# Gated cross-attention and mixture of experts on one core: token normalisation on ScalarE, and another order for the sixth and seventh batch

## The chip, the core and the metric

The kernel runs on one core of a Trainium2 chip. The core has TensorE (PE, matrix products, with a weight load of its own, PEld), VectorE (DVE), ScalarE (ACT), GpSimd (POOL) and SyncE (SP), which issues most DMAs. Each engine takes its instructions in program order and waits on semaphores for the others. Matrix products land in PSUM. The metric is the device time in microseconds of one execution, as the median of several runs. The program is all in fp32.

## The reference

`x` and `ctx` hold 8 batches of 256 rows with 512 columns. The rows are the channels of the attention and the tokens of the experts.

```python
x = x + tanh(g_xattn) * attention(layernorm(x), ctx, ctx)   # 16 heads of 16 channels, 512 positions, rotary
x = x + tanh(g_ffn) * moe(layernorm(x))                     # 8 experts, top 2 per token, hidden size 1024
# moe, per token:
#   logits = x @ gate_w ; top-2 softmax gives two weights
#   out = sum over the two experts of weight * ((silu(x @ w0[e]) * (x @ w1[e])) @ wo[e])
```

`layernorm` has no learned scale: it subtracts the mean over the 512 columns and divides by the root of variance plus 1e-5.

## The kernel before

**Attention.** A batch has 16 heads, taken in 4 units of 4 heads, and each unit goes through 4 blocks of 128 positions: a batch is 16 *steps*, and the attention has 128 steps, 0 to 127, written out by hand. In a step PE makes two groups of scores (`scores`, L551: four matmuls in each), whose maxima DVE takes (L559), and, five steps later (`LAG`), the scores again, transposed and less the maximum (`exponentials`, L590), of which ACT takes the exponential (L597). Both kinds use three PSUM buffers `s` in turn. A third product (`attend`, L607) sums values by exponentials. A scheduler holds a table `beside` of all other work: `do(step, place, fn, ...)` puts a function into a step at place 0, 1 or 2. For every step the program emits place 0, one group of exponentials and one of scores, place 1, the second group of each, and place 2. After step 127 only exponentials and what is left over are emitted, up to step 133.

`run` emits the entries of one place: products first, each then followed by its evacuation from PSUM, and the other functions after that. All products of this kind share one PSUM bank, `m`, of which there is one buffer: the next place's product waits until the last one has been evacuated by ACT or DVE.

**A batch's other work.** Let `t` be the batch's first step. Before it come the loads of `x` and `ctx` (`loads`, on SP's queue; `x` has three buffers, so the load waits until the batch three before has been normalised for its tokens), the mean and variance of `x` on DVE (`query_stats`), the normalisation for the query (`query_norm`; POOL computes the factors `rstd` and `less` in `Norm.scales`, and applies them, but for the first batch DVE applies them), products for k and q (`turn`, evacuated by ACT as `straight`), a swap of neighbouring rows by DMA on SP's queue, and the rotation on POOL (`rotate`). With `s = t + 24`, after the batch's last unit, follow `merge` (the output product, in halves of 256 columns; ACT scales it, POOL adds it to `x`, SP stores it), `token_stats` at s+5 (DVE statistics, POOL's `scales`), `token_norm` at s+6 (L160 on DVE, one 128x512 tile in each of two places, into `pay`, which has one buffer), `token_turn` (transposes, evacuated by ACT as `hT`), `choose` (logits) and the router: ten pieces (`largest`, `first_of`, `compare`, `count`, `shares`, `weigh`, `send`), nearly all small DVE instructions, the last of which scatter token rows with POOL's indirect DMAs into `rows`, sorted by expert.

The lists of strings such as `"9.1 11.1 13.1 14.1 ..."` give step after `s` and place of the two token turns, the logits and the ten pieces of the router. Batches 0 to 4 have them spread over s+9 to s+19. Batch 5 (the sixth, the last that "early" rows need) has them between s+9 and s+14, steps 113 to 118; batch 6 (the seventh) between s+9 and s+13, steps 129 to 133.

**Early rows.** At step 119 `start_early` loads the first 432 rows of expert 0, which batches 0 to 5 have filled, and clears four tiles `y` on DVE. `turn_early` transposes them in four pieces. After the attention the last batch is finished and routed while a generator (`go`) fills PE with matmuls of expert 0 on these rows. A loop for overflowing rows follows (it runs for no rows or few, but all engines meet there), then the gathers of the sums so far into `y`, and the experts' products, which are the second half of the span.

Of the kernel before, what the change touches and what calls it, by code (L numbers as in the profile page):

```python
# [8 lines left out]
FP = mybir.dt.float32  # L9
AF = mybir.ActivationFunctionType  # L10
ALU = mybir.AluOpType
# [3 lines left out]
P = 128  # L15
B, C, N = 8, 256, 512
# [5 lines left out]
CC = C // P  # L22
NCH = N // P
UNITS = 2 * NG
E, M = 8, 1024
# [11 lines left out]
AHEAD, EARLY, LATE = 6, 432, 160  # L37
# [3 lines left out]
ROW = N + 1 + E  # L41
# [8 lines left out]
def gated_cross_attention_moe(  # L50
# [89 lines left out]
    class Norm:  # L140


        def __init__(self, pool, part, srcs):
            self.srcs = srcs
            self.mv = pool.tile([P, CC, 2], FP, tag="mv" + part, name="mv")
            self.st = [pool.tile([P, 6], FP, tag=f"st{part}{c}", name="st") for c in range(CC)]
            self.rstd = pool.tile([P, CC], FP, tag="rstd" + part, name="rstd")
            self.less = pool.tile([P, CC], FP, tag="less" + part, name="less")

        def stats(self, c):  # L150
            nc.vector.bn_stats(self.st[c], self.srcs[c])
# [2 lines left out]
        def scales(self):  # L154
            nc.gpsimd.tensor_scalar(self.rstd, self.mv[:, :, 1], EPS, None, ALU.add)
            nc.gpsimd.tensor_tensor(self.rstd, self.rstd, neg_half, ALU.pow)
            nc.gpsimd.tensor_scalar(self.less, self.mv[:, :, 0], -1.0, None, ALU.mult)

        def apply(self, eng, dst, c):
            eng.tensor_scalar(  # L160
                dst, self.srcs[c], self.less[:, c : c + 1], self.rstd[:, c : c + 1], ALU.add, ALU.mult
            )

    w_even = ctx.enter_context(tc.tile_pool(name="w_even", bufs=1))

# [161 lines left out]
    with ExitStack() as fill:  # L327
# [79 lines left out]
        def bank():  # L407


            if not banks:  # L410
                banks.append(ps_1.tile([P, N], FP, tag="m", name="m"))
            return banks[0]
# [13 lines left out]
        def full(fn, *args):  # L426

            run([(fn, (*args, h)) for h in range(2)])
# [33 lines left out]
        def query_norm(b):  # L462
            xns[b] = r1.tile([P, CC, N], FP, tag="xn", name=f"xn{b}")
            norms[b].scales()
            for c in range(CC):
                norms[b].apply(nc.gpsimd if b else nc.vector, xns[b][:, c, :], c)

        def loads(b):
            load_x(b)
# [93 lines left out]
        def turn_half(src, h, at=None):  # L563

            ps = bank()[:, halves[h if at is None else at]]
            for i in range(2):
                nc.tensor.transpose(ps[:, i * P : (i + 1) * P], src(2 * h + i), ident)
            return ps
# [72 lines left out]

            return later

        def turn_back(b, g, h):
            ps = turn_half(lambda i: outs[b, g][:, i].rearrange("p j q d -> p (j q d)"), h)

            def later():
                if h == 0:
                    ats[b, g] = p1.tile([P, N], FP, tag=f"at{g}", name="at")
                nc.scalar.copy(ats[b, g][:, halves[h]], ps)  # L650

            return later
# [35 lines left out]

        def token_norm(b, c):
            if c == 0:  # L690
                pays[b] = p1.tile([P, CC, ROW], FP, tag="pay", name="pay")
            norms[b].apply(nc.vector, pays[b][:, c, :N], c)

        hTs = {}

# [18 lines left out]
        routes = {}  # L714


        def choose(b, c):
            lg = bank()[:, halves[c]][:, :E]
            hT = hTs.pop(c)
            for d in range(DC):  # L720
                nc.tensor.matmul(
                    lg,
                    lhsT=hT[:, d, :],
                    rhs=gw[:, d, :],
                    start=(d == 0),
                    stop=(d == DC - 1),
                )

            def later():
                if c == 0:  # L730
                    routes[b] = {"vals": small("logits", [P, CC, E])}
                nc.vector.tensor_copy(routes[b]["vals"][:, c, :], lg)

            return later
# [121 lines left out]
        def do(step, place, fn, *args):  # L856
            beside.setdefault((step, place), []).append((fn, args))
# [4 lines left out]
        for b in range(B):  # L862
            t = b * per_batch


            if b:
                do(t - 19, 1, loads, b)
                for c in range(CC):
                    do(t - 17, 1 + c, query_stats, b, c)
                do(t - 17, 2, query_norm, b)  # L870
                first = (-12, -10, -3, -1) if b == 1 else (-14, -12, -3, -1)
                for i, name_g in zip(first, group_turns):
                    for h, cols in enumerate(halves):
                        do(t + i + h, 2, turn, b, *name_g, cols)
                for i, name_g in zip((-4, -3, 4, 5), group_turns):
                    do(t + i, 2, rotate, b, *name_g)
            at = (2, 2, 3, 4) if b == 0 else (-8, -7, -6, 1) if b == 1 else (-10, -9, -8, 1)
            for mc, i in enumerate(at):
                if b:
                    do(t + i, 2, values, b, mc, halves[0])  # L880
                else:
                    do(i, 1 if mc == 3 else 2, values, b, mc, halves[mc == 1])
            for w in range(UNITS):
                u = UNITS * b + w
                s = t + w * NCH
                for mc in range(NCH):
                    do(s + LAG + 1 + mc, 1, attend, u, mc)
                for h in range(2):
                    do(s + NCH - 1 + h, 2 - h, lower, u, h)
                    if u + 1 < UNITS * B:  # L890
                        do(s + LAG + 5, 1 + h, normalise, u, h)
                        if w % 2:
                            do(s + LAG + 6 + h, 1 + h, turn_back, b, w // 2, h)
            if b + 1 == B:
                break
            s = t + per_batch + LAG + 3
            for c in range(CC):
                for h, cols in enumerate(halves):
                    do(s + 1 + 2 * c + h, 2, merge, b, c, cols)
                do(s + 5, 1 + c, token_stats, b, c)  # L900
                do(s + 6, 1 + c, token_norm, b, c)
            if b + 2 == B:
                at = "9.1 9.2 11.1 11.2 12.1 12.1 12.2 12.2 13.1 13.2 13.2 13.2 13.2"
            elif b + 1 == AHEAD:
                at = "9.1 11.1 11.2 12.1 12.1 12.2 12.2 12.2 13.1 13.2 13.2 14.1 14.1"
            else:
                at = "9.1 11.1 13.1 14.1 14.2 15.1 15.2 16.2 17.1 17.2 18.1 18.2 19.1"
            at = [(s + int(i[:-2]), int(i[-1])) for i in at.split()]
            for i, piece in zip(at, ((token_turn, b, 0), (token_turn, b, 1), (choose, b))):
                if b + 1 < AHEAD:  # L910
                    later = 1 if piece[0] is token_turn and piece[2] else 0
                    for h in range(2):
                        do(i[0] + h * later, 1 + h, *piece, h)
                else:
                    do(*i, full, *piece)
            for i, (fn, *args) in zip(at[3:], router):
                do(*i, fn, b, *args)
        do(-5, 2, turn, 0, "k", 0, whole)
        for c in range(CC):
            do(-5, 2, query_stats, 0, c)  # L920
# [19 lines left out]
        def start_early():  # L940
            prep.close()
            pool = fill.enter_context(tc.tile_pool(name="early", bufs=1, side="right"))
            early["pool"] = pool
            early["sg"] = fill.enter_context(tc.tile_pool(name="early_sg", bufs=2, side="right"))
            nc.vector.tensor_scalar(taken[:, 0:1], taken[:, 0:1], float(EARLY), None, ALU.max)
            early["rows"] = Rows(pool, 0, EARLY)
            early["y"] = [
                pool.tile([P, N], FP, tag=f"y{j}", name="y") for j, _ in early["rows"].tiles
            ]
            for y in early["y"]:  # L950
                nc.vector.memset(y, 0.0)

        do(t - 1, 1, start_early)
        def turn_early():
            banks.clear()
            early["rows"].turn(bank, nc.scalar.copy)

        for at in ((t + 5, 1), (t + 5, 2), (t + 11, 2), (t + 12, 2)):
            do(*at, turn_early)

        held = []
# [26 lines left out]
        with tc.manual_schedule():  # L988
# [31 lines left out]
            go(1)  # L1020
            full(token_turn, b, 1)
            go(1)
            full(choose, b)
            for fn, *args in router:
                if fn is count:
                    go(4)
# [79 lines left out]
        late_p = ctx.enter_context(tc.tile_pool(name="late", bufs=1, reuse_waits="tile"))  # L1106
        fx = ctx.enter_context(tc.tile_pool(name="fx", bufs=2, reuse_waits="tile"))
        with tc.manual_schedule():
            early["rows"].residuals(early["y"])
            ws_next = matrices(1, w_odd)  # L1110
            late = Rows(late_p, EARLY, LATE)
            following = Rows(fx, ROWS, CAP)
            for _ in work:
                pass
            late.turn_all(get_x, nc.vector.tensor_copy)
# [107 lines left out]
```

## Time and profile before

| what | value |
|---|---|
| median of 3 runs | 1432.69 us (1431.8 to 1433.01) |
| profiled execution | 1431.27 us, span 1429.6 us |
| mean granted TensorE clock | 0.987 |
| PE busy | 1380.8 us, 97% of the span |
| DVE, ACT, POOL busy | 581.4, 412.1, 309.6 us |
| first scores (step 0) | 19.73 us after the start |
| last step with scores (127) starts | 640.15 us |
| first early matmul | 667.04 us |
| PE continues behind the overflow loop | 703.93 us |

A row of the timeline gives the start, the duration, engine, line, operation, the tiles written and read, their shape, how many like instructions were merged, and in brackets how long the engine stood idle before it and what released it. A row of the waits gives engine and line that waited, on what, the total, how many times, and the longest. A row of busy times of a stretch gives its bounds and length, then PE, PEld, DVE, ACT and POOL busy with the number of instructions, the granted clock, the share of DMA and GB/s.

### The profile page before, as it was taken

To read this page: it belongs to the slowest core of one execution; us is meant where nothing else is said; L and a number is where in the kernel's file an instruction comes from. 1 tells how busy PE (TensorE), PEld (TensorE's weight loads), DVE (VectorE), ACT (ScalarE), POOL (GpSimd) and SP (SyncE) were. 2 spreads that over 40 slices of the span, in tenths; PEclk is the share of its full clock that TensorE was granted. 3 is DMA by queue.
4 is the path that set the end of the run, shared out by engine and by line. 5 is a ranking of instruction groups with operands and counts; after the bars stand their busy time and mean duration, and the time that the engine had idled before them with its cause. 6 is when DMAs were issued, how large, how long until landed. Compare 5 with 4: busy or idle time off the path is not lost. (4 is left out here: it accounts for less than half of the span.)

```text
span 1429.6 us, 18158 instructions
## 1 busy us (share of the span) xinstructions
PE 1380.8 (97%) x7380; PEld 766.2 (54%) x7380; DVE 581.4 (41%) x1058; ACT 412.1 (29%) x617; POOL 309.6 (22%) x361
## 2 busy tenths in 40 slices
PE   5999999999999999998999999999999999999996
PEld 2333343434434343333447876858768577585772
DVE  5666767686767777672313111121211211112110
ACT  1556555555555555354100100101001010010000
POOL 6231515243341415211201102011020110100101
PEclk9999999999999999899999999999999999999998
DMA  6600512021111101010354234033340332310100
GB/s 216 216 19 23 175 69 88 16 65 40 46 52 46 52 16 61 25 47 38 145 180 150 80 125 141 1 141 128 118 133 17 140 128 103 121 47 16 43 1 28
DMA packets 49061, 117.76 MB, mean 82 GB/s; under 512 B 6122, under 2 KB 7146, under 8 KB 48976
## 3 DMA queue, kind: packets, MB, share of 16 engines
q1 hardware_dynamic: 40688, 91.26, 18.3%
q0 software_dynamic: 8288, 25.32, 4.9%
q8 instruction: 59, 0.97, 0.3%
q14 instruction: 26, 0.21, 0.0%
HBM read 78.51 MB, written 30.91 MB: 77 GB/s over the span
## 5 line engine op out<-in xcount | busy, mean ns | idle before, releaser
L559 DVE TENSOR_REDUCE nm<-s 128x2 f32<-128x1024 f32 x256 | 312.9, 1224 | 145.2 <-PE s L551 142.2
L597 ACT ACTIVATE e<-s 128x1024 f32<-128x1024 f32 x256 | 261.2, 1023 | 190.1 <-PE s L551 148.7
L551 PE MATMUL s<-k,q 32*128 32x512 f32 x1024 | 288.9, 651 | 6.9 <-POOL q L508 6.1
L590 PE MATMUL s<-qa,k 32*128 32x512 f32 x1024 | 287.1, 649 | 0.0
L257 PE MATMUL u<-hT,w 128*128 128x272 f32 (+1 forms) x960 | 233.4, 387 | 1.5 <-DVE act L271 1.5
L257 PE MATMUL g<-hT,w 128*128 128x272 f32 (+1 forms) x960 | 233.4, 387 | 0.0
L270 ACT ACTIVATE sg<-g 128x272 f32<-128x272 f32 (+1 forms) x120 | 46.8, 391 | 611.5 <-PE g L257 608.0
L287 PE MATMUL po<-wo,act 128*32 128x128 f32 (+1 forms) x976 | 221.0, 427 | 0.0
L271 DVE TENSOR_TENSOR act<-sg,u 128x272 f32<-128x272 f32 (+1 forms) x120 | 51.4, 429 | 368.4 <-PE u L257 368.4
L257 PEld LDWEIGHTS g<-hT,w 128*128 128x128 f32 x960 | 179.4, 190 | 37.2 <-issue 2.9
L257 PEld LDWEIGHTS u<-hT,w 128*128 128x128 f32 x960 | 179.4, 190 | 36.6 <-DVE act L271 1.7
L306 POOL DMA_INDIRECT out_x<-y,xt x41 | 39.6, 967 | 570.7 <-DVE y L298 532.8
L287 PEld LDWEIGHTS po<-wo,act 128*32 128x32 f32 (+1 forms) x976 | 99.3, 148 | 102.5 <-issue 102.3
L607 PE MATMUL av<-e,vones 128*32 128x512 f32 x1024 | 139.0, 615 | 0.0
L590 PEld LDWEIGHTS s<-qa,k 32*128 32x128 f32 x1024 | 76.8, 185 | 74.7 <-issue 64.1
L298 DVE SCALAR_TENSOR_TENSOR y<-po,xt,y 32x128 f32<-32x128 f32 (+1 forms) x61 | 32.8, 538 | 180.5 <-PE po L287 180.2
L551 PEld LDWEIGHTS s<-k,q 32*128 32x128 f32 x1024 | 76.9, 186 | 17.1 <-ACT e L597 7.4
L607 PEld LDWEIGHTS av<-e,vones 128*32 128x32 f32 x1024 | 20.3, 109 | 98.9 <-issue 98.9
L677 POOL TENSOR_TENSOR x<-x,mrg 128x512 f32<-128x512 f32 x14 | 17.9, 1276 | 200.0 <-ACT mrg L673 200.0
L238 POOL DMA_INDIRECT y<-out_x,xt x41 | 40.9, 997 | 68.4 <-issue 32.3
L257 PE MATMUL s<-hT,w 128*128 128x432 f32 x128 | 48.4, 529 | 2.4 <-DVEq L1051 2.4
L489 ACT ACTIVATE straight<-m,col 128x256 f32<-128x256 f32 (+1 forms) x60 | 29.3, 489 | 68.7 <-DVE o L635 24.3
(135 smaller groups left out, 995.8 us busy)
## 6 DMA issues: line engine op xcount, KB each, us to landing
w<-in_w SPq DMA_DIRECT2D x16, 2048.0 KB, 10.4
wo<-in_wo SPq DMA_DIRECT2D x8, 2048.0 KB, 9.4
rows<-nobody SPq DMA_DIRECT2D x8, 1042.0 KB, 7.3
xt<-rows SPq DMA_DIRECT2D x32, 260.5 KB, 4.7
swapped<-straight SPq DMA_DIRECT2D x64, 128.0 KB, 2.0
ctx<-in_kv SPq DMA_DIRECT2D x8, 512.0 KB, 4.3
x<-in_x SPq DMA_DIRECT2D x16, 256.0 KB, 2.8
out_x<-x SPq DMA_DIRECT2D x16, 256.0 KB, 2.0
```

The source lines that it names most:

```text
L238: gather = nc.gpsimd.indirect_dma_start(out=y[: at.shape[0], :], out_offset=None, in_=out_rows, in_offset=bass.IndirectOffsetOnAxis(ap=at, ...
L257: nc.tensor.matmul(ps[:, :step], lhsT=w[:, d, mc * P : (mc + 1) * P], rhs=self.hT[:, d, lo : lo + step], start=(d == 0), stop=(d == DC - 1),)
L270: nc.scalar.activation(sg, gu[0][:, :step], AF.Silu)
L271: nc.vector.tensor_tensor(self.act[:, mc, lo : lo + step], sg, gu[1][:, :step], ALU.mult)
L287: nc.tensor.matmul(po[i * space : i * space + n, :w], lhsT=self.act[:, mc, j * P : j * P + n], rhs=wout[:, mc, i * w : (i + 1) * w], start ...
L298: nc.vector.scalar_tensor_tensor(part, po[i * space : i * space + n, :w], wt[:n, j, :], part, ALU.mult, ALU.add,)
L306: scatter = nc.gpsimd.indirect_dma_start(out=out_rows, out_offset=bass.IndirectOffsetOnAxis(ap=self.ids[j], axis=0), in_=y[:n, :], in_offs ...
L551: nc.tensor.matmul(ps[:, j, :], lhsT=q[sl, i * P : (i + 1) * P], rhs=k[sl, :], start=True, stop=True,)
L559: nc.vector.tensor_reduce(nm[:, i, at : at + SLOT + 1 : SLOT], ps, AX.X, ALU.max, negate=True)
L590: nc.tensor.matmul(ps[:, j, :], lhsT=ks[u][sl, mc * P : (mc + 1) * P], rhs=qas[u][sl, :], start=True, stop=True,)
L597: nc.scalar.activation(es[u, mc][:, 2 * jp : 2 * jp + 2, :], ps, AF.Exp, scale=float(HD**-0.5))
L607: nc.tensor.matmul(avs_[u][slot(j), :], lhsT=vones[b % 2][:, mc, g * HG + 2 * j + par, :], rhs=e[:, j, :], start=(mc == 0), stop=(mc == NC ...
```

## The change

- `Norm` computes one factor more on POOL, `bias` = `less` x `rstd`, and `apply` on ACT is an Identity activation with that bias and `rstd` as scale.
- `token_norm` goes from DVE to ACT, and from s+6 to s+7. The first batch's `query_norm` goes from DVE to ACT as well; those of the other batches stay on POOL. `pay` gets two buffers.
- `loads`, `query_stats` and `query_norm` of batches 1 to 7 come two steps later (`t`-17 and `t`-15).
- Batch 5's token turns, logits and router get the steps that batches 0 to 4 have, with the two sends at s+19 and s+20 (steps 123, 124).
- Batch 6 has its merges whole (512 columns) at s and s+1, statistics at s+2, both norms at s+3, turns at s+4 and s+5, logits at s+6 and the router at s+7 to s+10 (steps 120 to 130). For that, the second half of the last `turn_back` comes one step earlier and uses the other half of the bank.
- `start_early` goes from step 119 to 124 behind these sends; the four early turns go from 125, 125, 131 and 132 to two each in 129 and 131. The clearing of the four `y` moves behind the overflow loop.

```diff
+            self.bias = pool.tile([P, CC], FP, tag="bias" + part, name="bias")
...
             nc.gpsimd.tensor_scalar(self.less, self.mv[:, :, 0], -1.0, None, ALU.mult)
+            nc.gpsimd.tensor_tensor(self.bias, self.less, self.rstd, ALU.mult)
 
         def apply(self, eng, dst, c):
-            eng.tensor_scalar(
-                dst, self.srcs[c], self.less[:, c : c + 1], self.rstd[:, c : c + 1], ALU.add, ALU.mult
-            )
+            less, rstd, bias = (t[:, c : c + 1] for t in (self.less, self.rstd, self.bias))
+            if eng is nc.scalar:
+                eng.activation(dst, self.srcs[c], AF.Identity, bias=bias, scale=rstd)
+            else:
+                eng.tensor_scalar(dst, self.srcs[c], less, rstd, ALU.add, ALU.mult)
...
-                norms[b].apply(nc.gpsimd if b else nc.vector, xns[b][:, c, :], c)
+                norms[b].apply(nc.gpsimd if b else nc.scalar, xns[b][:, c, :], c)
...
-        def turn_back(b, g, h):
-            ps = turn_half(lambda i: outs[b, g][:, i].rearrange("p j q d -> p (j q d)"), h)
+        def turn_back(b, g, h, other=False):
+            ps = turn_half(
+                lambda i: outs[b, g][:, i].rearrange("p j q d -> p (j q d)"), h, h ^ other
+            )
...
-                pays[b] = p1.tile([P, CC, ROW], FP, tag="pay", name="pay")
-            norms[b].apply(nc.vector, pays[b][:, c, :N], c)
+                pays[b] = p2.tile([P, CC, ROW], FP, tag="pay", name="pay")
+            norms[b].apply(nc.scalar, pays[b][:, c, :N], c)
...
-        def choose(b, c):
-            lg = bank()[:, halves[c]][:, :E]
+        def choose(b, c, at):
+            lg = bank()[:, halves[at]][:, :E]
...
-                do(t - 19, 1, loads, b)
+                do(t - 17, 1, loads, b)
                 for c in range(CC):
-                    do(t - 17, 1 + c, query_stats, b, c)
-                do(t - 17, 2, query_norm, b)
+                    do(t - 15, 1 + c, query_stats, b, c)
+                do(t - 15, 2, query_norm, b)
...
                         if w % 2:
-                            do(s + LAG + 6 + h, 1 + h, turn_back, b, w // 2, h)
+                            last = h and (b, w) == (B - 2, UNITS - 1)
+                            do(s + LAG + 6 + h - last, 1 + h, turn_back, b, w // 2, h, last)
...
             s = t + per_batch + LAG + 3
-            for c in range(CC):
-                for h, cols in enumerate(halves):
-                    do(s + 1 + 2 * c + h, 2, merge, b, c, cols)
-                do(s + 5, 1 + c, token_stats, b, c)
-                do(s + 6, 1 + c, token_norm, b, c)
             if b + 2 == B:
-                at = "9.1 9.2 11.1 11.2 12.1 12.1 12.2 12.2 13.1 13.2 13.2 13.2 13.2"
-            elif b + 1 == AHEAD:
-                at = "9.1 11.1 11.2 12.1 12.1 12.2 12.2 12.2 13.1 13.2 13.2 14.1 14.1"
+
+                for c in range(CC):
+                    do(s + c, 2, merge, b, c, whole)
+                    do(s + 2, 1 + c, token_stats, b, c)
+                    do(s + 3, 2, token_norm, b, c)
+                    do(s + 4 + c, 2, full, token_turn, b, c)
+                    do(s + 6, 1 + c, choose, b, c, 1 - c)
+                at = "7.1 7.1 7.2 7.2 8.1 9.1 9.1 9.2 9.2 10.1"
             else:
-                at = "9.1 11.1 13.1 14.1 14.2 15.1 15.2 16.2 17.1 17.2 18.1 18.2 19.1"
...
+                for c in range(CC):
+                    for h, cols in enumerate(halves):
+                        do(s + 1 + 2 * c + h, 2, merge, b, c, cols)
+                        do(s + 9 + 2 * c + (c and h), 1 + h, token_turn, b, c, h)
+                    do(s + 5, 1 + c, token_stats, b, c)
+                    do(s + 7, 1 + c, token_norm, b, c)
+                    do(s + 13, 1 + c, choose, b, c, c)
+                at = "14.1 14.2 15.1 15.2 16.2 17.1 17.2 18.1 18.2 19.1"
+                if b + 1 == AHEAD:
+                    at = at[:-9] + "19.2 20.1"
+            for i, (fn, *args) in zip(at.split(), router):
+                do(s + int(i[:-2]), int(i[-1]), fn, b, *args)
...
-            for y in early["y"]:
-                nc.vector.memset(y, 0.0)
-
-        do(t - 1, 1, start_early)
+
+        do(t + 4, 2, start_early)
...
-        for at in ((t + 5, 1), (t + 5, 2), (t + 11, 2), (t + 12, 2)):
+        for at in ((t + 9, 1), (t + 9, 2), (t + 11, 1), (t + 11, 2)):
             do(*at, turn_early)
...
-            full(choose, b)
+            run([(choose, (b, c, c)) for c in range(CC)])
...
         with tc.manual_schedule():
+            for y in early["y"]:
+                nc.vector.memset(y, 0.0)
             early["rows"].residuals(early["y"])
```

More of the change, by code (lines that the diff above doesn't have):

```diff
@@ L896, in gated_cross_attention_moe @@
             s = t + per_batch + LAG + 3
-            for c in range(CC):
-                for h, cols in enumerate(halves):
-                    do(s + 1 + 2 * c + h, 2, merge, b, c, cols)
-                do(s + 5, 1 + c, token_stats, b, c)
-                do(s + 6, 1 + c, token_norm, b, c)
-            if b + 2 == B:
-                at = "9.1 9.2 11.1 11.2 12.1 12.1 12.2 12.2 13.1 13.2 13.2 13.2 13.2"
-            elif b + 1 == AHEAD:
-                at = "9.1 11.1 11.2 12.1 12.1 12.2 12.2 12.2 13.1 13.2 13.2 14.1 14.1"
-            else:
-                at = "9.1 11.1 13.1 14.1 14.2 15.1 15.2 16.2 17.1 17.2 18.1 18.2 19.1"
[L908 to L917, printed above, removed]
+            if b + 2 == B:
+                for c in range(CC):
[5 more added lines that the diff above has]
+                at = "7.1 7.1 7.2 7.2 8.1 9.1 9.1 9.2 9.2 10.1"
+            else:
+                for c in range(CC):
[10 more added lines that the diff above has]
+                do(s + int(i[:-2]), int(i[-1]), fn, b, *args)
         do(-5, 2, turn, 0, "k", 0, whole)
```

## The prediction

> **What bounds the kernel now.** I read the page first, then the waits, the busy time of single stretches, and the timeline around the places that the diff touches. From the page:
>
> ```profile
> PE 1380.8 (97%) x7380; PEld 766.2 (54%) x7380; DVE 581.4 (41%) x1058; ACT 412.1 (29%) x617; POOL 309.6 (22%) x361
> PEclk9999999999999999899999999999999999999998
> ```
>
> PE is busy almost throughout, so only what delays PE counts. In the timeline I took the start of every step (eight L551 matmuls each). A full step of attention takes 4.74 us in nearly all of steps 17 to 114; what departs from that is the material. Step 47 lasts 6.65, and so do 31, 63, 79 and 111 (6.59, 6.63, 6.63, 6.62); step 95 lasts 7.65 and 96 lasts 5.34. Steps 115 to 118 take 8.09, 7.11, 7.38 and 6.74. Step 63, by busy time of the stretch and by timeline:
>
> ```profile
> 314.58:321.22 6.64, 5.35 (x36) 2.13 (x35) 6.57 (x9) 2.67 (x4) 3.62 (x3) 1.00 0.39 90
> ...
> 314.33 1.47 DVE L160 TENSOR_SCALAR pay<-x,less,rstd 128x512 f32<-128x512 f32 x1 [1.43 <-POOL less L157]
> 317.01 1.26 POOL L508 TENSOR_TENSOR q<-a,swapped 128x512 f32<-128x512 f32 x1
> 317.08 0.29 DVE L635 TENSOR_TENSOR o<-m,rec 128x128 f32<-128x128 f32 x1
> 317.29 1.27 DVE L160 TENSOR_SCALAR pay<-x,less,rstd 128x512 f32<-128x512 f32 x1
> 317.47 0.47 ACT L489 ACTIVATE straight<-m,col 128x256 f32<-128x256 f32 x1 [3.01 <-DVE o L635]
> 318.00 0.44 PE L567 MATMUL m<-ident,o 128*128 128x128 f32 x2 [1.29 <-ACT straight L489]
> 318.37 1.13 PE L590 MATMUL s<-qa,k 32*128 32x512 f32 x4
> 318.91 1.13 PE L551 MATMUL s<-k,q 32*128 32x512 f32 x4
> ```
>
> The first row's third pair is DVE: 6.57 of 6.64 us. Two normalisations of tokens (1.47 and 1.27, behind a wait of 1.43 for POOL's `less`) hold back the evacuation of the one PSUM bank "m", and PE stands 1.29 us; then its two score groups run one after the other, which costs the rest of the 1.9.
>
> The fourth and fifth place, in the sixth batch's routing and at the attention's end:
>
> ```profile
> 578.90 2.67 PE L721 MATMUL m<-gw,hT 128*128 128x8 f32 x16 [1.33 <-DVE qa L578]
> 583.68 1.02 ACT L597 ACTIVATE e<-s 128x1024 f32<-128x1024 f32 x1 [5.43 <-PE s L551]
> 588.75 1.02 DVE L741 SCALAR_TENSOR_TENSOR rest<-hot,logits 128x16 f32<-128x16 f32 x1
> 592.63 0.40 PE L778 MATMUL m<-both,before 128*128 128x16 f32 x2 [1.89 <-DVE both L769]
> ...
> 652.46 0.66 PE L567 MATMUL m<-ident,pay 128*128 128x128 f32 x4 [1.53 <-ACT hT L702]
> 671.38 0.63 PE L567 MATMUL m<-ident,o 128*128 128x128 f32 x4 [1.48 <-DVE o L635]
> ...
> 573.40:602.70 29.30, 25.82 (x130) 10.14 (x128) 18.16 (x48) 9.40 (x12) 5.43 (x6) 0.77 0.00 1
> ```
>
> Steps 115 to 118 are that last stretch: waits of 1.33 and 1.89 for the crowded router, and a clock of 0.77 (its records show half clock from 579.9 to 586.8 and from 593.6 to 600.4; also 477.5 to 481.0 and 661.9 to 665.3).
>
> **What the Trainium skill says.** SBUF — State Buffer, "Who interferes with whom": GpSimd and a VectorE `tensor_scalar` in a two-port mode exclude each other for a whole instruction. The trace agrees: beside POOL's work the token normalisation takes 1266 to 1474 ns, with POOL idle (638.46) 550. ScalarE: Activation LUTs, "What ACT_TABLE_LOAD costs": 186 ns + 0.833 per element, and 93 per pointer operand, an estimate of 0.80 us for 512 elements with two; the nearest row, the merge of 128x512 with two pointers, has 777 ns. TensorE: Matmul & The Clock Gate, "What's actually happening": half clock follows an idle window of some 3.4 us; here it came after waits of 1.3 to 1.9, but not after each of them.
>
> **The change part by part.**
>
> *Token normalisation on ACT at s+7 (six boundaries).* DVE loses 2 x 1.37, 6.57 to 3.83 us of work, under PE's 4.74; the wait for `less` goes too. PE gets back the excess over 4.74: 1.85+1.91+1.89+1.89+1.88 = 9.42 in five, and 2.91+0.60 = 3.51 in steps 95 and 96 (half clock included): 12.93. ACT gains 2 x 0.78. In the first half of s+7 it has copy 0.37 + 0.78 + exponential 1.02 = 2.17, in the second 0.475 + 0.78 + 1.02 = 2.28, against half a step of 2.37. Behind it in ACT's order stand the exponentials, whose buffer the next scores need; the first norm runs while PE makes the scores, the second delays an exponential by about 0.65, and PE then has attend (0.99) and a transpose (0.37) to do. From nothing to 0.78 is possible; I take 0.2 each: 1.2. The new `bias` is one POOL instruction like `less`, 0.24. Behind it waits the rotation of q, which the next batch's first score needs. That q is done at 318.27; without the stall it is wanted at 305.51 (start of step 61) + 4.32 + 2 x 4.74 = 319.31. With 0.3 more it has 0.7 us of cover: nothing, up to 1 if POOL runs into something.
>
> *Loads and query statistics two steps later.* x waits in SP's queue for ACT's second norm instead of DVE's; behind it are ctx and the swaps of q1, which are rotated four steps on. x lands in 2.8 us and is wanted 1.5 steps (7 us) after. POOL's norm of the query moves from s+7 to s+9, with two idle steps behind. All nothing, except in the first batch: there the statistics of batch 1 (2 x 0.87) ran at 18.6 to 20.3 before DVE's first maxima, and now fall between them, where DVE has 2.36 us in a step of 3.0. I charge 0.5 (0 to 1.7).
>
> *First batch's query on ACT.* DVE began at 11.02 and PE at 11.66. Now `bias` (0.25), then 0.78 each: first product near 12.2, q and so the first score 0.5 later. k's path leaves DVE earlier, but q is the wait at 19.73 (6.12). Cost 0.5 (0.2 to 1).
>
> *Sixth and seventh batch, steps 112 to 126.* Old 81.17 us (558.98 to 640.15). New, by content: a light step here takes 4.67, whatever is in it up to 4.2 us of PE work. 112: 4.88 as it is; 113: 4.74; 114, 115, 116, 118, 119 (with the second turn back, moved in from 120), 122: 6 x 4.67 = 28.02; 117 with both logits (2.14 scores + 0.99 attend + 1.9): 5.1; 120 and 121 each with a whole merge (1.98): 5.44 and 5.6; 123 with both norms on ACT (1.56 in front of one exponential): 5.2; 124: 4.67; 125: 4.5; 126 with the seventh's logits: 5.7. Sum 73.85: gain 7.3, if no half clock comes; it would take 1.7 or 3.4 back each. A copy of `pay` more (two buffers) keeps the seventh's norm from waiting for the sixth's sends at 123 and 124.
>
> *From step 127 to the first early matmul.* Old 26.89. The seventh's turns and logits (4 x 0.33 twice, 1.9) and the 1.53 wait have left; but four early turns now stand in 129 and 131, each behind ACT's copy (0.59) of the one before, and in 129 the count as well. By the old pieces: 3.86, 4.19, 5.0, 3.6, 4.15, 3.2, 1.0: 25.0, gain 1.9 (-1 to 5). The early rows leave by 124 and land some 11 us later, two steps before the first turn.
>
> *The tail.* The router no longer holds DVE to 670.26, so `o` comes in time: 1.4 back of 1.48. The last batch's norm on ACT starts 0.25 later and takes 0.24 more on PE's path (683.00, where it waits 0.29 already): cost 0.45. The four memsets (0.49 each) go behind the loop's barrier, in front of the gathers at 704.57, whose sums are first added at 731: hidden; without that cover, 2 us.
>
> Sum: 12.93 - 1.2 - 0.5 - 0.5 + 7.3 + 1.9 + 1.4 - 0.45 = 20.9. Everything after 704 shifts whole. From the profiled execution's 1431.27 that is 1410.4; it lies 1.4 under the median, so 1411.8.
>
> **Rivals.** *The wait moves to ACT or POOL.* The 0.65 of slack isn't there, or q comes late: all 1.56 of each boundary reach PE, 1.36 more than charged, six times 8.2: 1420. For it: two halves at 2.17 and 2.28 of 2.37, and q's 0.7 us. Against: PE's own 1.36 of work before it needs the buffer. *The stage of the two batches stays crowded:* the gains of 7.3 and 1.9 fall out: 1421. For it: sixth's router, seventh's statistics, norms and merges within 118 to 124. Against: other batches route in steps of 4.65 to 4.85. *Better:* no half clock anywhere, light ends: the last stage gains 5 and ACT costs nothing: 1407 or less. *Slower:* half clock at the boundaries. If ACT makes PE stand as long as the router did (1.33) and a 6.8 us window of half clock (3.4 lost) follows, a boundary costs 4.73. Six are 28.4 instead of 12.93, +15.5 against the other 9.2 of gain (7.3+1.9+1.4-1.45): 1439. It decides from five boundaries of six. For it: 477.5 shows such a window at one. Against: five like waits brought none. *Not as described:* the ACT branch hangs on an identity test of the engine; if it failed, the operation would still be put on ACT. Small.
>
> **How the numbers follow.** The forecast (1407 to 1418) has 0.55, one of the first two rivals (1418 to 1428) 0.20, better 0.10, no change within 0.2% (some 2.9 us, about what a measurement can tell) 0.04, slower 0.11. Range 1404 to 1422: it holds the forecast, most of better, and the lower part of the rivals. Faster 0.85, same 0.04, slower 0.11.
>
> **What would show it.** Steps 31, 47, ... 111 at 4.7 to 5.0; no DVE row for `pay` in the attention, ACT rows of some 0.78 instead; steps 115 to 118 near 5 each with clock 1.0; no wait of `m<-ident,o` near 670; the first score 0.5 later. It is wrong if PE waits for `e` or q at the boundaries, if half clock lies in 600 to 665, or if PE waits for ACT's `hT` in 129 and 131.

## The result, and the profile after

The changed kernel takes 1418.84 us (1418.54 to 1422.71, 6 runs) beside 1432.24 of the kernel before (1431.09 to 1433.95, 6 runs): a ratio of 0.9913, 95% interval 0.9899 to 0.9927. It is faster by 13.4 us by the medians (12.5 by the ratio), where 20.9 had been worked out. A second set of runs gave 1419.90 and 0.9914 (0.9896 to 0.9932).

The changed kernel's profiled execution took 1422.71 us, the longest of its six. From its page, the engines' busy time and the granted clock by slices:

```profile
PE 1379.9 (97%) x7372; PEld 764.6 (54%) x7372; DVE 561.3 (39%) x1040; ACT 426.2 (30%) x633; POOL 312.2 (22%) x377
PEclk8999999999999999999999999999999999999998
```

The norms have moved from DVE (20 us less) to ACT (14 more), and PE is where it was. The busy time of step 63, then the groups of instructions of the two norms that ACT took over (busy, mean ns, idle before and its releaser):

```profile
315.84:320.68 4.84, 4.84 (x35) 1.94 (x37) 3.00 (x6) 3.60 (x5) 3.72 (x3) 1.00 0.16 58
...
L164 ACT ACTIVATE pay<-x,bias,rstd 128x512 f32<-128x512 f32 x16 | 12.8, 811 | 4.2 <-POOL bias L159 4.1
L164 ACT ACTIVATE xn<-x,bias,rstd 128x512 f32<-128x512 f32 x2 | 1.5, 808 | 1.1 <-POOL bias L159 1.1
```

The step takes 4.84 instead of 6.64, and PE is busy in all of it. An ACT norm takes 811 ns. So far the times are those of the forecast. Steps 117 and 118, by busy time and by the timeline:

```profile
575.52:591.41 15.89, 13.02 (x71) 5.12 (x69) 7.58 (x15) 4.89 (x6) 3.50 (x3) 0.79 0.00 1
...
577.83 1.27 POOL L512 TENSOR_TENSOR q<-a,swapped 128x512 f32<-128x512 f32 x1
579.27 2.11 DVE L1116 MEMSET y<- 128x512 f32 x4 [3.54 <-POOL q L512]
581.29 1.16 DVE L563 TENSOR_REDUCE nm<-s 128x2 f32<-128x1024 f32 x1
582.37 0.15 DVE L738 COPY logits<-m 128x8 f32<-128x8 f32 x1
582.57 1.45 PE L727 MATMUL m<-gw,hT 128*128 128x8 f32 x8 [2.87 <-DVE logits L738]
```

The two steps take 15.89 us, where 9.77 was forecast. L1116 are the four clearings of `y`, which the source puts behind the overflow loop, 100 us later. They stand in the middle of the attention and wait 3.54 us for POOL's last rotation. A maximum (L563) and the copy of the logits out of the bank `m` (L738) come behind them on DVE. PE waits 2.87 us for that copy, and half clock (the records grant 0.5 of TensorE's clock) lies on 583.1 to 589.9.

It is no accident of timing. DVE takes its instructions in the order of the compiled program, and in the next profile of the same kernel (`same_again`) the clearings stand ahead of the same maximum, again after a wait of 3.54. So the build moved them, though both ends of the move lie in parts whose order is written out by hand. Its rule for this was not looked into. What the clearings wait for is probably room: `start_early` gives back the pools of the rotation just before it opens that of `y`. No run tested that.

The two profiles against each other, stage by stage, from the starts of the steps (gains are positive, in us). The boundaries are steps 31, 47, ... 111, where the stall of step 63 stood, and the steps behind the first five:

| stage | forecast | profiled pair | seen in other profiles |
|---|---|---|---|
| start to step 5 | -1.0 | -2.8 | -0.8 where both are on half clock for as long (`clear_behind` against `clear_moved`) |
| boundaries (31, 32, 47, 48 ... 96, 111) | 11.7 | 11.6 | 10.0 without the half clock of the kernel before at 477.5 |
| steps 37, 38 | 0 | -1.6 | half clock 194.0 to 197.4, not in the next profile |
| 112 to 126 | 7.3 | 2.1 | 6.4 to 8.3 with the clearing elsewhere |
| 127 to the first early product | 1.9 | 1.7 | 1.0 to 2.1 |
| early product to behind the barrier | 0.95 | 1.3 | 1.3 to 1.7 |
| after | 0 | -3.8 | half clock 692.3 to 695.7 and 753.7 to 757.1, some 3.4 of it |

With 0.1 from step 88 this makes 8.6, the difference of the spans (1429.6 and 1421.0). The medians are 13.4 apart, since the profiled execution is a long one.

### The profile page after: what moved, and what is told of

Same layout as the page of the kernel before. It is cut to its first block, busy times and chain, and to the rows that moved or that the text cites. A ratio compares the mean times of both kernels' runs of the same rounds, so it can differ in the third digit from the quotient of the medians.

```text
span 1421.0 us, 18152 instructions
## 1 busy us (share of the span) xinstructions
PE 1379.9 (97%) x7372; PEld 764.6 (54%) x7372; DVE 561.3 (39%) x1040; ACT 426.2 (30%) x633; POOL 312.2 (22%) x377
## 3 DMA queue, kind: packets, MB, share of 16 engines
q1 hardware_dynamic: 40688, 91.26, 18.3%
## 5 line engine op out<-in xcount | busy, mean ns | idle before, releaser
L563 DVE TENSOR_REDUCE nm<-s 128x2 f32<-128x1024 f32 x256 | 313.2, 1225 | 162.3 <-PE s L555 158.9
```

Source lines behind the costliest of these rows:

```text
L563: nc.vector.tensor_reduce(nm[:, i, at : at + SLOT + 1 : SLOT], ps, AX.X, ALU.max, negate=True)
```

## Experiments

**Where the missing 7 us went.** Each run is compared with the kernel before in its own set: 1431.81 us for `same_again`, `clear_at_132`, `clear_moved` and `norm_only`, 1432.83 for `clear_behind`, `norm_back_132`, `spread_logits` and `first_on_dve`, and 1433.16 for the last four. `same_again` is the changed kernel itself.

> The changed kernel unaltered, beside the others on one chip. Its profile had 1421.0 us of span and 1422.71 us in a group of runs with a median of 1418.84. If the 3.9 us between them are half-clock windows that fall differently from run to run, this profile shows another number of windows, and span less the half of all half-clock time before the last products (10.2 us in the first profile) agrees with 1410.8 within 1 us. If they are something else, the windows are the same and the waits differ. Time expected: 1418 to 1420.

1419.90 us (1416.29 to 1422.54). Its profiled execution took 1417.1, with 20.5 us of half clock before the last products, against 27.3 in the first (half of it is 13.7; the 10.2 in the expectation was added up wrongly). The windows at 194 and 753.7 are gone. Span less half of the half-clock time is 1407.4 in one and 1405.2 in the other: the windows of half clock account for 3.4 of the 5.6 us between the two executions, and the stated 1 us was missed. From step 1 to 126 the two agree to 0.02 us in every step but 37, 38, 117 and 118, where half clock lies.

`clear_at_132` takes the clearing of `y` out of its place behind the loop:

```diff
+        def clear_early():
+            for y in early["y"]:
+                nc.vector.memset(y, 0.0)
+
+        do(t + 12, 1, clear_early)
...
-            for y in early["y"]:
-                nc.vector.memset(y, 0.0)
             early["rows"].residuals(early["y"])
```

> The changed kernel with the clearing of the four y put into step 132 of the written order, where DVE has little to do, instead of behind the loop. Theory A: the clearing was compiled into step 117, where it waits for POOL's last rotation in front of a maximum; PE's wait of 2.87 us, the rest of DVE's 2.11 us of clearing and one window of half clock (3.4 us) go, steps 117 and 118 fall from 8.45 and 7.44 to some 5.2 and 4.7, and the time falls by 5 to 6.5 us, to 1412 to 1414. Rival B: the stage is crowded by the sixth batch's router itself and the clearing only fills a gap: steps 117 and 118 still take over 13 us together, and the time falls by less than 1.5 us.

1414.28 us (1413.77 to 1414.91), ratio 0.9874 (0.9856 to 0.9892): 5.6 us under the changed kernel. Busy time of steps 117 and 118:

```profile
573.43:585.04 11.61, 11.61 (x71) 4.55 (x69) 5.90 (x11) 4.90 (x6) 3.50 (x3) 0.85 0.01 1
```

The two steps take 11.61 instead of 15.89, and PE waits nowhere, with a clock of 0.85. The crowded router (rival B) is refuted: without the clearing, PE doesn't wait for the same router in the same steps.

`clear_moved` makes the same edit in the kernel before, the other way round: its clearing goes from `start_early` (step 119) behind the loop.

> The kernel before with one edit of the change, the clearing of the four y put behind the loop in the source. Theory A: it lands early here too, in front of some maximum at about step 114 to 117 and behind POOL's rotation, so that DVE is held there, and this kernel is slower than before by 2 to 6 us. Rival B: it fills a gap, and the time stays within 1 us of before.

1435.42 us, ratio 1.0027 (1.0018 to 1.0035): 3.6 us slower. Its timeline:

```profile
593.68 0.48 DVE L1108 MEMSET y<- 128x512 f32 x1 [2.71 <-POOL q L508]
596.37 0.61 PE L778 MATMUL m<-both,before 128*128 128x16 f32 x2 [4.42 <-DVE both L769]
```

The clearing jumped to step 117 here as well, behind the same rotation, and PE's wait for `both` grew from 1.89 to 4.42. So this one edit of the change is a loss in both kernels. Its profile places 1.5 of the 3.6 us in steps 112 to 126 (82.64 instead of 81.17); where the rest lies isn't shown.

`clear_behind` holds the clearing to its place in the source, ahead of the last part written by hand:

```diff
-        with tc.manual_schedule():
-            for y in early["y"]:
-                nc.vector.memset(y, 0.0)
+        for y in early["y"]:
+            tc.keep_in_program_order(nc.vector.memset(y, 0.0))
+        with tc.manual_schedule():
             early["rows"].residuals(early["y"])
```

> The changed kernel with the four clearings held to their place in the source, just ahead of the loop's barrier, where nothing but early products runs (DVE: 737 of its order instead of 576). Theory A: as with the clearing in step 132, 1413.5 to 1415.5: steps 117 and 118 clean, and the clearing hidden. Rival: next to the barrier it shows, by up to its own 2 us: 1415.5 to 1417.

1414.58 us (1412.66 to 1417.42) beside 1432.83, ratio 0.9872 (0.9855 to 0.9889). Busy time of steps 117 and 118, and the rows of the tile's clearing:

```profile
577.82:587.78 9.96, 9.96 (x70) 4.36 (x68) 5.88 (x11) 4.88 (x6) 3.49 (x3) 1.00 0.01 2
...
L1115 DVE MEMSET y<- x4: 485/485/485, 682.2 to 683.8; 128x512 f32 x4
```

9.96 us is within 0.2 of the forecast's 9.77, and steps 112 to 126 take 73.10 where 73.85 was worked out. The clearing at 682 costs nothing that shows. That is what the change would have been, had the program run as its source reads.

**What made the stall at the boundaries.** The forecast gave it to DVE's load. `norm_only` puts into the kernel before only this: `token_norm` on ACT at s+7, and loads, statistics and the query's norm two steps later.

> The kernel before with the norm of the tokens on ACT at s+7 and the loads and statistics of the query two steps later; the first batch's query stays on DVE, pay keeps one buffer, sixth and seventh batch and early rows stay as they were. By the prediction's sum: 12.93 - 1.2 - 0.5 = 11.2 us faster, 1421. If the gain of the boundaries is given back elsewhere (ACT in front of the exponentials, q late), it is under 7 us. By the changed kernel's trace each boundary gave 1.6 us, 9.7 in all six with 3.2 in the one with half clock.

1424.87 us (1422.51 to 1426.70), ratio 0.9949 (0.9934 to 0.9963): 6.9 us. A boundary and the step behind it take 4.76 and 4.98. The gain is less than 11.2. Of that, 1.6 was the half clock at 477.5, which `clear_moved`, with the boundaries of the kernel before, hasn't at its step 95 (6.62). Why the rest of the profile's 10.0 doesn't show in the median stays open.

`norm_back_132` is `clear_at_132` with the norms of the tokens back on DVE, in the new places:

```diff
-            norms[b].apply(nc.scalar, pays[b][:, c, :N], c)
+            norms[b].apply(nc.vector, pays[b][:, c, :N], c)
```

> The changed kernel with the clearing in step 132 and the norms of the tokens back on DVE, at the new place s+7, where POOL's less is long there. If DVE's work in the step (2 x 1.37 us beside 3.8) makes the stall, each boundary takes 6.2 to 6.6 us again and the time is 8 to 11 us over the one with the clearing in 132 alone, 1422 to 1425. If the wait for less (1.43) made it, a boundary takes under 5.3 and the time is within 3 us of it, under 1417.5.

1412.75 us (1408.89 to 1417.17), ratio 0.9874 (0.9853 to 0.9895), level with ACT. The boundaries take 4.76 and 4.74. So it need not be ACT. But eleven of the twelve norms took 0.54 us here instead of some 1.37, so that DVE had less to do too (3.38 us in step 63). Two edits of the kernel before go on from there. `moved_only` leaves the norms on DVE and moves them to the new place, with the loads:

```diff
-                do(s + 6, 1 + c, token_norm, b, c)
+                do(s + 7, 1 + c, token_norm, b, c)
...
-                do(t - 19, 1, loads, b)
+                do(t - 17, 1, loads, b)
```

(`query_stats` and `query_norm` go to t-15 as well.) `act_at_6` has the norm on ACT at s+6, and these where they were.

> The kernel before with the norm of the tokens left on DVE and moved from s+6 to s+7, and the loads and statistics of the query two steps later; nothing else. New theory, from the kernel with the norms back on DVE: the place alone takes the stall away, because less is ready [...]; boundaries at 4.8, pay rows of some 540 ns, and a time 7 to 10 us under before, at least as good as the same edit on ACT (6.9). Old theory, that DVE has too much to do in the step: boundaries at 6 or more, less than 3 us gained.

1420.43 us (1418.11 to 1421.65) beside 1433.16, ratio 0.9903 (0.9885 to 0.9920), 12.7 us where 7 to 10 were expected. Step 63 by busy time, and DVE's two norms in the timeline; then step 111 by busy time, and the two norms there (shortest, median and longest in ns):

```profile
313.76:318.52 4.76, 4.76 (x35) 1.86 (x35) 4.13 (x6) 2.89 (x4) 3.43 (x3) 1.00 0.15 55
...
316.12 1.43 DVE L160 TENSOR_SCALAR pay<-x,less,rstd 128x512 f32<-128x512 f32 x1
318.94 0.54 DVE L160 TENSOR_SCALAR pay<-x,less,rstd 128x512 f32<-128x512 f32 x1
...
544.33:549.10 4.77, 4.77 (x36) 1.87 (x35) 4.14 (x6) 2.89 (x4) 4.69 (x4) 1.00 0.15 55
...
L160 DVE TENSOR_SCALAR pay<-x,less,rstd x2: 1257/1346/1436, 546.7 to 549.5; 128x512 f32<-128x512 f32 x2
```

At step 63 one norm still takes 1.43 us, beside POOL (the expected 540 ns came in one of the two), and PE stands nowhere. At step 111 both are as slow as in the kernel before, 1.44 and 1.26 us, and the step takes 4.77 with PE busy in all of it. So the load of the two norms on DVE was not what made the stall. A move of one step, on DVE, gained as much as the whole change. Norm and loads moved together here; they weren't tried apart.

> The kernel before with the norm of the tokens on ACT at the old place s+6, loads and statistics where they were; nothing else. New theory: ACT then waits for less in DVE's stead, in front of an exponential, so that a part of the stall stays: boundaries of steps s+6 and s+7 together 0.5 to 2 us over 9.5, and the gain is under 7 us. Old theory: freeing DVE is what counts, and the gain is that of ACT at s+7, 6.9 or more.

1431.42 us, ratio 0.9987 (0.9977 to 0.9997): 1.7 us. Step 62 by busy time, POOL's rotation of k and its factor with ACT's norm in the timeline, the norm's row of the waits, and DVE's row in the kernel before:

```profile
312.40:318.92 6.52, 5.85 (x37) 2.12 (x36) 4.46 (x9) 3.27 (x5) 6.01 (x10) 1.00 0.01 3
...
313.88 1.52 POOL L518 TENSOR_SCALAR k<-a,half_col,spare_col 128x512 f32<-128x512 f32 x2
316.92 0.19 POOL L159 TENSOR_TENSOR bias<-less,rstd 128x2 f32<-128x2 f32 x1
317.15 0.81 ACT L164 ACTIVATE pay<-x,bias,rstd 128x512 f32<-128x512 f32 x1 [2.51 <-POOL bias L159]
...
ACT pay L164 <- POOL bias L159: 20.2, 8, 4.1
...
DVE pay L160 <- POOL less L157: 10.0, 7, 1.5
```

The stall has changed its engine and gone one step ahead: step 62 takes 6.52 instead of 4.74, step 63 takes 4.76. ACT waits 20.2 us in all for POOL's `bias`, as DVE waited 10.0 for `less` in the kernel before, with the exponentials behind it. At s+6 POOL's factors are not ready, since its rotation of k is ahead of them in its order; at s+7 they are, for either engine. At s+7 DVE has also evacuated `o` before the norm (at 314.10 in `moved_only`); how much of the gain is due to that alone wasn't separated.

**The second half of the change alone.** `order_only` has all norms on DVE, those of batches 0 to 5 at s+6 with the loads where they were, the clearing in step 132, and sixth, seventh batch and early rows as changed. `pay` has two buffers, and POOL still makes `bias`, which nothing reads.

> The changed kernel's second half alone: sixth and seventh batch and early rows in the new order, the clearing in step 132, but all norms on DVE, those of batches 0 to 5 at s+6 and loads where they were. Boundaries 31 to 111 at 6.6 as before; steps 112 to 126 near 75 us (81.2 before), the last maxima to the first early product 25 (26.9). By the prediction's terms 7.3 + 1.9 + 1.4 = 10.6 us faster than before, by the trace of the changed kernel with clean steps 6.4 + 1.6 + 1.7 = 9.7.

1417.46 us (1414.05 to 1422.61, 5 runs), ratio 0.9878 (0.9858 to 0.9897): 15.7 us by the medians. Steps 112 to 126 take 74.61, the last maxima to the early product 24.84. But the boundaries take 5.67 to 5.71, and not 6.6, which is 5.6 us that the order of the batches didn't bring. The other 10.1 are what was expected. The timeline at one:

```profile
315.70 0.55 DVE L166 TENSOR_SCALAR pay<-x,less,rstd 128x512 f32<-128x512 f32 x1 [1.42 <-POOL less L158]
315.75 0.19 POOL L159 TENSOR_TENSOR bias<-less,rstd 128x2 f32<-128x2 f32 x1
315.89 1.47 POOL L508 TENSOR_TENSOR a<-straight,f 128x512 f32<-128x512 f32 x1
317.74 1.15 DVE L166 TENSOR_SCALAR pay<-x,less,rstd 128x512 f32<-128x512 f32 x1
```

The wait for `less` is there as before (1.42), but the norm behind it takes 0.55 instead of 1.47. Between `less` and the rotation POOL now has 0.2 us of `bias`, so that DVE comes first, and POOL's 1.27 becomes 1.47. Two other runs agree: at s+7 the norms take 0.54 in five boundaries of six with `bias` (`norm_back_132`), and without it (`moved_only`) the first of the two takes 1.40 to 1.45 in all six. That `bias` decides the order is argued from this; it wasn't tried alone.

**Smaller matters.** `spread_logits` is `clear_at_132` with one of the sixth batch's two groups of logits a step earlier (116 and 117).

> The changed kernel with the clearing in step 132, and the sixth batch's two groups of logits in steps 116 and 117 instead of both in 117. In the profile with the clearing in 132, half clock for 3.4 us still lies on 117, though PE waits nowhere there. If it comes from 16 products of 8 columns standing together, it goes: steps 116 to 118 sum to 15.0 to 15.4 instead of 16.27 and the time falls by 1 to 1.7. If the window falls by chance, the time is the same within 0.7.

1416.25 us (1414.12 to 1418.32), ratio 0.9883 (0.9866 to 0.9899): no gain. Steps 116 to 118 take 14.54, without half clock, as do those of `clear_behind` with both groups in 117 (14.63): the window there falls by chance. `first_on_dve` is `clear_at_132` with `nc.vector` for the first batch's query.

> The changed kernel with the clearing in step 132 and the first batch's query normalised on DVE as before. By the prediction's step the first score comes 0.5 us sooner (the profiles on ACT have 21.98, 21.99 and 22.04, a kernel with the old start 21.47): 21.5, and the time falls by 0.5. If ACT cost more at the start, as the first pair of profiles suggests (2.26), it falls by about 2.

1413.07 us (1409.99 to 1415.08), ratio 0.9870 (0.9854 to 0.9887), not told from 0.9874. The first score came at 19.62, but with full clock where the others had half, as in the first profile of the kernel before; so the 0.5 was not measured. `best` has all that looked good by profile: `clear_at_132`, both norms on DVE, and batch 1's loads and statistics where they were.

> The changed kernel with the clearing in step 132, all norms on DVE (of the tokens at s+7, the first batch's query as before), and batch 1's loads and statistics where they were before. Boundaries at 4.76 and 4.74 instead of 4.77 and 4.98, start as before. Expected 1410 to 1413, some 2 us under the one with the clearing in 132 alone and 7 to 9 under the changed kernel. If the engine doesn't matter at all, it is level with the one with norms back on DVE (1412.75).

1415.70 us (1410.53 to 1420.49), ratio 0.9877 (0.9851 to 0.9903): no better than `clear_at_132`, and above the 1410 to 1413 expected. Its profiled execution, at 1410.62, has steps 112 to 126 in 72.97 and all boundaries at 4.76 and 4.74, but its six runs spread over 10 us.

## Why the prediction was right, and where not

The direction and the range (1404 to 1422) held. The forecast's own range, 1407 to 1418, was missed by 0.8 us, and of 20.9 us some 13 came. The time lies where the prediction had put its first two rivals (1418 to 1428), but the cause is neither of theirs.

**Boundaries.** The size was right in the profiled pair (11.6 of 11.7), the reason was not. "DVE loses 2 x 1.37, 6.57 to 3.83 us of work, under PE's 4.74" fails: with both norms on DVE one step later and as slow as before, the step takes 4.77 (`moved_only`, step 111), and with ACT in the old place the stall stands one step ahead, at 6.52 (`act_at_6`). A full engine in one stretch (6.57 of 6.64) had been read as work in excess of the step. In the lines of step 63 only the first norm stands ahead of `o`; the second (317.29) comes behind it and cannot hold it back. What held `o` back was a wait of 1.43 for POOL's factors, which ended just before the stretch began and so isn't in its busy time, and then the first norm's 1.47 us beside POOL. Where that norm took 0.55 and the wait stayed (`order_only`), the stall fell from 1.9 to 0.95; where the wait was gone, PE stood nowhere, even with the norm at 1.44. The clause that "the wait for `less` goes too" was the cause, not an addition. ACT's charge of 0.2 was right: 0.24 in each (steps 32, 48, 80 at 4.98). The 1.6 of half clock at 477.5 was counted as gain, but belongs to one execution, so that the close agreement of 11.6 and 11.7 is in part luck.

**q's cover, loads two steps later.** At no boundary does PE wait for q, `e`, x or ctx. So the rival of the wait that moves to ACT or POOL did not come.

**First batch and batch 1.** Forecast 1.0 lost; the first pair shows 2.8. Most of that is clock: the profile of the kernel before had full clock from 9.9 to 16.7, and others were on half clock until 27 to 28. Among those, two with the old start reach step 5 at 40.58 and 40.63 (`act_at_6`, `clear_moved`), two with the moved statistics and the old query at 40.74 and 41.11 (`moved_only`, `norm_only`), and one with both moves at 41.45 (`clear_behind`). So the new start costs about 0.8: 0.1 to 0.5 for the statistics and 0.3 to 0.7 for ACT's query, where 0.5 was charged for each. These are single executions.

**Sixth and seventh batch.** This is the step that cost the forecast most. "Four memsets go behind the loop's barrier ... hidden; without that cover, 2 us" took the source's order for the program's. They were compiled into step 117, and what they cost wasn't their own 2 us but the wait for POOL in front of them, 3.54, and what it brought on: 5.6 us by `clear_at_132`. The working of the stage itself was right: 73.85 forecast, 72.91 to 74.74 in seven profiles with the clearing elsewhere. Much of what went there is half clock: all five profiles with the old router, where PE waits 1.33 us and then 1.89 or more, have 10.2 to 13.7 us of it in this stage; those seven, where PE doesn't wait, have none or 3.4. The rival of the crowded stage, which had nearly this time (1421), was wrong in its cause.

**From 127 to the barrier.** 25.0 forecast, 25.18 and 24.80 measured to the first early product. Some 0.8 of the gain is the half clock of the kernel before at 661.9: `clear_moved` and `norm_only`, without it, take 26.07 instead of 26.89. PE waits 0.68 and 1.37 us for ACT's `hT` in steps 129 and 131. The prediction had named that as a sign of being wrong, and its sum held nevertheless. The wait for `o` at 671 is gone, and the stretch to the barrier is 1.3 shorter (0.95).

**Behind the barrier.** Forecast to shift whole; half clock at 692 and 754 took some 3.4 in this execution, and one such window some 1.7 in the next. The rival with half clock at the boundaries did not come: none has a window there in any profile after the change.

With the clearing put right the gain is 17.5 to 18.3 us (0.9874, 0.9872), against 20.9. Of the rest 1.6 is the half clock at 477.5; the remainder, probably other windows of half clock, wasn't accounted for.

**Open.** `norm_only` and `moved_only` differ by 0.24 us at each of six boundaries, 1.4 in all, and their profiled executions took 1422.51 and 1421.65; yet their intervals (0.9934 to 0.9963 and 0.9885 to 0.9920) are further apart than that. They ran in different sets and on different chips. Why the runs of one kernel spread over up to 10 us was not settled; windows of half clock are the largest thing seen to differ between two executions, and they explained 3.4 of 5.6.

## What to carry to other kernels

An engine that is busy for the whole of a stretched step need not be its cause: look whether the instruction that stretches it waits for something, and try it one place later before giving it to another engine. An instruction that the source puts late, and that depends on nothing late, may be compiled early. Look at the compiled order: the cost is then not the instruction's own duration but the wait in front of it and all that stands behind. Before a stall's cost is taken from one execution, take out what half clock added to it.

## What the runs showed of the hardware

- With 0.19 us of POOL's work between `less` and the rotation, a DVE norm that waited for `less` took 0.55 us instead of 1.47, the rotation's first instruction 1.47 instead of 1.27, and the boundary was 0.93 shorter (`order_only` beside the kernel before). In these rows the one that started first kept its short time.
- Half clock came with no wait of PE at all (578.8 in `clear_at_132`, PE busy in 11.61 of 11.61 us) and stayed away after waits of 1.3 (five of the six boundaries of the kernel before). In the same program it falls in other places from one execution to the next, in pieces of 3.4 us or multiples of that; one piece makes a busy step some 1.65 us longer (step 118 with 6.31 instead of 4.67).
